# Attention loop of a fused cross-attention and quantised FFN kernel: another order of the steps over four groups in flight

## The chip, the cores and the metric

The kernel runs on one core of a Trainium2 chip. Its time is the device time of one execution, in microseconds (us); a smaller number is better. Five engines take part, each with a queue of its own that it works through: PE (TensorE, matrix products and transposes), DVE (VectorE), ACT (ScalarE), POOL (GpSimd), and SP, which here only issues transfers between HBM and the on-chip memory. Products land in PSUM[...]; everything else on the chip lives in SBUF.

## What is computed

The input `x` has 2 x 2048 tokens of 512 values, the context 2 x 128 tokens. A cross-attention is added to `x`, and then a feed-forward layer whose activations and weights are rounded to integers:

```python
x = x + xattn(layernorm(x), ctx, Wq, Wkv)
x = x + ffn(layernorm(x), w_gate, w_up, w_down)

# xattn: softmax((h @ Wq) @ key.T / sqrt(512)) @ value,  key, value = split(ctx @ Wkv)
# ffn:
x = act_qdq(x)                                  # 16-bit integers, one scale: max |x| over the tensor
up = act_qdq(x @ lpbq_dequant(w_up).T)          # weights: 4 bits in blocks of 32
gate = act_qdq(x @ lpbq_dequant(w_gate).T)
gate = act_qdq(gate * fixed_qdq_u16(sigmoid(gate)))
return act_qdq(gate * up) @ lpbq_dequant(w_down).T
```

The scale of `act_qdq(x)` needs the largest magnitude of the whole normalised tensor, so no product of the FFN can start before the last token has gone through the attention.

## The kernel before

Tokens are worked on in eight groups of 512 (`NG = 8`, `TG = 512`), each held as four tiles of 128 tokens (`NJ = 4`). The program has four stages one after the other: attention (to about 191 us), the gate product (to 469 us), the up product (to 745 us), the down product (from 794 us). This case is about the first.

For one group `g` the attention stage does this. `front` transposes the group's tokens on PE (`xt`, L271) and copies them to SBUF on ACT (`xT`, L272); DVE takes means and variances (L276, L277), and POOL raises them to the power -0.5 (L259). `scores` multiplies with the folded key matrix (`sc`, L288), takes row maxima on DVE (`nmx`, L296, L297), exponentials with row sums on ACT (`e`, L301), and reciprocals of the sums on DVE (`den`, L309). `attend` transposes the exponentials on PE (`pe`, L393), copies them on ACT (`eT`, L395), multiplies with the values (`po`, L399), and adds the result to the tokens on DVE (L400), which also yields row sums (`total`). Then it forms the negative mean on DVE (L411), squares on ACT with row sums (L416), the variance on DVE (L424), its root on POOL (L259) and the shift on DVE (L426). `finish` writes the normalised group `h` on ACT (L433), takes its largest magnitude on DVE (`hmax`, through the helper at L155), transposes it on PE (`ht`, L442) and copies it on ACT (`hT`, L443).

In program order a turn `g` of the loop is: load group `g+2`; scores of `g`; front of `g+1`; three steps of weights; `finish` of `g-1`; `attend` of `g`; three steps of weights. After the loop stands `finish` of group 7.

The "steps of weights" are slices of a generator (`split_weights`, called through `split_rows`) that rounds the gate weights in four blocks of 384 rows. One block is: load (L161), block maxima on DVE (L155), scale and reciprocal (L167, L169), integers (`wi`, L171), back to floats (`w`, L173), three times four transposes on PE and a copy on ACT (`wt`, L179; `wsp`, L180), three splitting operations on DVE (L182, L184, L187) and a store (L189). Six of them take about 1.75 us of DVE each. The same generator works through up and down weights inside the gate stage.

The order of a queue isn't the program's: a scheduler of the language places the instructions of each engine at build time, by priorities and its own estimate of when things are ready. What stands behind what on an engine is therefore read from the built queues. Buffers of the pools are handed out in turn, and a new tile waits until the tile that had its buffer has been read. The PSUM pools of this stage are `ps_t` (two buffers of two banks: `xt`, `ht`), `ps_s` (two of one bank: `sc`, `pe` and `wt`) and `ps_o` (two of one bank: `po`).

After the stage, `over_partitions` reduces `hmax` (L136, POOL L138), `act_scale` makes the scale (L147, L149), group 0 is rounded on DVE (`hi`, L494) and split into the parts of the product (`parts_g`, L221 to L224), while ACT rounds other groups (L500) and makes the first parts (L222). The first matrix product of the gate stage is L479. The last eight of twelve gate weight tiles are loaded at the end of the attention (L471), since their memory is that of the attention's buffers.

Of the kernel before, what the change touches and what calls it, by code (L numbers as in the profile page):

```python
# [62 lines left out]
P = 128  # L63
# [6 lines left out]
EPS = 1e-5  # L70
# [5 lines left out]
def tile_xattn_ffn(  # L76
# [48 lines left out]

    hmax = const.tile([P, NG], F32, name="hmax")
    gmax = const.tile([P, NG * NK], F32, name="gmax")
# [26 lines left out]
    def abs_max(col, src, axis=AX.X):  # L154
        nc.vector.tensor_reduce(col, src, axis, ALU.max, apply_absolute_value=True)  # L155

    def split_weights(pool, psum, src, dst, name):
# [18 lines left out]
        for b in range(3):  # L176
            pt = psum.tile([P, D], F32, tag="tr", name=f"wt_{name}_{b}")
            for c in range(ND):
                nc.tensor.transpose(pt[:, ts(c, P)], w[:, b, ts(c, P)], ident)  # L179
            nc.scalar.copy(ws[:, 2, b, :], pt)  # L180
            yield
# [49 lines left out]
    with ExitStack() as c0:  # L231

        with ExitStack() as c1:
# [20 lines left out]
            nc.gpsimd.memset(mean, 1.0 / D)  # L254
            gate_steps = split_rows(wk1, ps_s, w_gate, wg_d, "g")
            xts = {}
            def inverse_root(ve, name):
                rstd = sm.tile([P, NJ], F32, tag=f"rstd{name[0]}", name=f"rstd_{name}")
                nc.gpsimd.tensor_tensor(rstd, ve, mhalf, ALU.pow)  # L259
                return rstd  # L260

            def front(g):

                xt = xts[g]
                xT = wk2.tile([P, NJ, ND, P], F32, tag="xT", name=f"xT_{g}")
                for j in range(0, NJ, 2):
                    pt = two_banks(f"xt_{g}_{j}")
                    pt4 = pt.rearrange("p (j c k) -> p j c k", j=2, c=ND)
                    for i in range(2):
                        for c in range(ND):  # L270
                            nc.tensor.transpose(pt4[:, i, c, :], xt[:, j + i, ts(c, P)], ident)  # L271
                    nc.scalar.copy(xT[:, j : j + 2], pt4)  # L272
# [7 lines left out]
                return xT, inverse_root(ve, f"x{g}")  # L280

# [104 lines left out]

            def attend(g, e, rden):

                b = g * TG // S
                xt = xts[g]  # L390
                pe = ps_s.tile([P, NJ, P], F32, tag="tr", name=f"pe_{g}")
# [3 lines left out]
                nc.scalar.copy(eT, pe)  # L395
                total = sm.tile([P, NJ], F32, tag="total", name=f"total_{g}")
                for j in range(NJ):
                    po = ps_o.tile([P, D], F32, tag="o", name=f"po_{g}_{j}")
# [9 lines left out]
                    )  # L408
                nc.sync.dma_start(out=x1_d[g], in_=xt)
                nmean = sm.tile([P, NJ], F32, tag="nmean", name=f"nmean_{g}")  # L410
                nc.vector.tensor_scalar(nmean, total, -1.0 / D, None, ALU.mult)  # L411
                h = wk2.tile([P, NJ, D], F32, tag="h", name=f"h_{g}")
                squares = sm.tile([P, NJ], F32, tag="squares", name=f"squares_{g}")
                for j in range(NJ):

# [6 lines left out]
                    )  # L422
                ve = sm.tile([P, NJ], F32, tag="ve2", name=f"ve2_{g}")
                nc.vector.tensor_scalar(ve, squares, 1.0 / D, EPS, ALU.mult, ALU.add)  # L424
                rstd = inverse_root(ve, f"h{g}")
                nc.vector.tensor_tensor(nmean, nmean, rstd, ALU.mult)  # L426
                return h, nmean, rstd

            def finish(g, h, shift, rstd):

                xt = xts.pop(g)
                for j in range(NJ):
                    nc.scalar.activation(  # L433
                        h[:, j, :], xt[:, j, :], AF.Identity, bias=shift[:, j : j + 1], scale=rstd[:, j : j + 1]
                    )
                abs_max(hmax[:, g : g + 1], h, AX.XY)
                for j in range(0, NJ, 2):
# [6 lines left out]

            last = None
            for g in range(NG):
                if g + 2 < NG:
                    xts[g + 2] = load_x(g + 2)
                if g:
                    soft = scores(g, *ahead)  # L450
                if g + 1 < NG:
                    ahead = front(g + 1)
                advance(gate_steps, 3)
                if last is not None:
                    finish(g - 1, *last)
                last = attend(g, *soft)
                advance(gate_steps, 3)
            finish(NG - 1, *last)
            advance(gate_steps, 100)


# [317 lines left out]
```

## Time and profile before

| What | us |
|---|---|
| Median of three runs | 1062.96 (1062.78 to 1064.39) |
| The profiled execution's own time | 1063.58 |
| Its span in the trace | 1061.8 |
| First residual addition of group 0 (L400) | 49.87 |
| End of the last `h` (L433, group 7) | 184.74 |
| First product of the gate stage (L479) | 190.88 |
| First product of the up stage | 470.08 |
| First product of the down stage (L742) | 793.6 |

The squares (L416) of groups 0 to 7 begin at 56.62, 74.34, 93.67, 112.50, 130.59, 149.66, 166.62 and 177.22 us. They serve below as marks of the pace of the loop: each group has exactly one such set, and it stands in the middle of the group's chain.

The profile of one execution is read as follows. A timeline line gives start, duration, engine, line, operation, output and inputs, and in brackets how long the engine stood idle before it and what released it. A windows line gives, for a stretch of time, the busy time of each engine in it with the number of instructions, the clock granted to PE as a share of full speed, and the load of the transfer engines. A waits line adds up how long one kind of instruction let its engine stand idle for another. The three latter stages are bound by PE, which is busy for 271 of the 274 us from 191 to 465 us; the attention stage isn't.

### The profile page before, as it was taken

What the parts mean: (1) busy time and instruction counts of PE and PEld (TensorE: products, weight loads), DVE (VectorE), ACT (ScalarE), POOL (GpSimd) and SP (SyncE); (2) the same over time, 40 slices, a digit from 0 to 9 for tenths busy, and PEclk for the clock granted to TensorE, in tenths of its full rate; (3) what the DMA queues carried; (4) which work ended last, traced back from release to release, by engine and by line L of the source; (5) the groups of instructions that cost most, each with busy time, mean ns of one, the idle gap of its engine ahead of it and who ended that gap; (6) DMA issues with size and microseconds to landing.
All of it is one profiled execution on the core that took longest, in us unless ns stands there. A gap on an engine that the chain in (4) does not pass through costs nothing. (4 is left out here: it accounts for less than half of the span.)

```text
span 1061.8 us, 11414 instructions
## 1 busy us (share of the span) xinstructions
PE 949.2 (89%) x4320; PEld 772.3 (73%) x4320; DVE 793.9 (75%) x897; ACT 542.0 (51%) x582; POOL 72.2 (7%) x63
## 2 busy tenths in 40 slices
PE   6977876899999989999799999999019999999998
PEld 6756663688888878877678888888008888888886
DVE  4577944989998979544777897779458887888782
ACT  2277577532333323225888889888325344443441
POOL 0101010000000000000000000000001112111211
PEclk9988887899999999999899999999559999999999
DMA  8177632977887697887988988889989766766520
GB/s 326 31 291 268 237 135 81 392 304 307 336 351 243 251 328 288 318 323 319 383 286 332 380 319 318 324 323 353 352 269 307 234 196 196 233 190 215 169 76 34
DMA packets 118110, 281.83 MB, mean 265 GB/s; under 512 B 5408, under 2 KB 72992, under 8 KB 105632
## 3 DMA queue, kind: packets, MB, share of 16 engines
q1 hardware_dynamic: 117232, 278.42, 72.0%
q0 software_dynamic: 288, 1.57, 0.4%
q10 hardware_dynamic: 528, 1.05, 0.3%
q8 instruction: 34, 0.56, 0.2%
q14 instruction: 28, 0.23, 0.1%
HBM read 147.85 MB, written 133.17 MB: 265 GB/s over the span
## 5 line engine op out<-in xcount | busy, mean ns | idle before, releaser
L742 PE MATMUL yq<-wd,parts_o 128*128 128x512 f32 x768 | 182.0, 393 | 48.7 <-ACT parts_o L222 48.7
L742 PEld LDWEIGHTS yq<-wd,parts_o 128*128 128x128 f32 x768 | 145.8, 190 | 79.8 <-ACT parts_o L222 49.1
L479 PE MATMUL q_u<-parts_u,wu 128*128 128x512 f32 x768 | 192.4, 393 | 9.8 <-ACT u L595 8.5
L479 PE MATMUL q_g<-parts_g,wg 128*128 128x512 f32 x768 | 195.1, 394 | 4.5 <-ACT parts_g L222 4.5
L479 PEld LDWEIGHTS q_u<-parts_u,wu 128*128 128x128 f32 x768 | 144.7, 189 | 42.8 <-ACT u L595 11.5
L479 PEld LDWEIGHTS q_g<-parts_g,wg 128*128 128x128 f32 x768 | 143.8, 189 | 35.1 <-issue 4.9
L523 ACT ACTIVATE g<-q_g 128x512 f32<-128x512 f32 x96 | 57.5, 601 | 170.6 <-PE q_g L479 165.7
L483 PE MATMUL e_g<-parts_g,wg 128*128 128x512 f32 x384 | 103.6, 391 | 0.0
L483 PE MATMUL e_u<-parts_u,wu 128*128 128x512 f32 x384 | 103.2, 391 | 0.3 <-DVE u L596 0.3
L524 DVE CUSTOM_DVE_ANT_0 g<-g,e_g 128x512 f32<-128x512 f32 x96 | 64.6, 683 | 37.3 <-PE e_g L483 36.9
L746 PE MATMUL ye<-wd,parts_o 128*128 128x512 f32 x384 | 92.2, 389 | 0.0
L588 DVE SCALAR_TENSOR_TENSOR pi<-gi,k_p,sq 128x2048 int16<-128x2048 int16 x24 | 56.3, 2347 | 45.9 <-ACT sq L564 45.9
L483 PEld LDWEIGHTS e_u<-parts_u,wu 128*128 128x128 f32 x384 | 72.5, 189 | 15.9 <-DVE u L596 0.7
L483 PEld LDWEIGHTS e_g<-parts_g,wg 128*128 128x128 f32 x384 | 72.3, 188 | 15.0
L746 PEld LDWEIGHTS ye<-wd,parts_o 128*128 128x128 f32 x384 | 72.1, 188 | 14.9
L750 ACT ACTIVATE yqs<-yq,q_o 128x512 f32<-128x512 f32 x32 | 22.1, 690 | 117.6 <-PE yq L742 117.6
L596 DVE TENSOR_TENSOR u<-u,e_u 128x1024 f32<-128x1024 f32 x48 | 58.5, 1218 | 13.7 <-ACT u L595 13.4
L754 DVE SCALAR_TENSOR_TENSOR y<-ye,e_o,qx 128x512 f32<-128x512 f32 x32 | 24.1, 752 | 57.6 <-PE ye L746 48.3
L752 POOL TENSOR_TENSOR qx<-yqs,x 128x512 f32<-128x512 f32 x32 | 50.0, 1562 | 226.0 <-ACT yqs L750 226.0
L222 ACT CAST parts_o<-sa_o 128x1536 fp32r<-128x1536 int16 x32 | 47.1, 1475 | 34.9 <-PE ye L746 30.8
L595 ACT ACTIVATE u<-q_u 128x1024 f32<-128x1024 f32 x48 | 48.1, 1017 | 31.0 <-PE q_u L479 27.9
L734 DVE SCALAR_TENSOR_TENSOR oi<-p,k_o,ui 128x1536 int16<-128x1536 int16 x32 | 58.0, 1819 | 4.1 <-ACT ui L730 2.2
(165 smaller groups left out, 1293.8 us busy)
## 6 DMA issues: line engine op xcount, KB each, us to landing
parts_d<-parts_g SPq DMA_DIRECT2D x8, 3072.0 KB, 10.9
gate_d<-g SPq DMA_DIRECT2D x24, 1024.0 KB, 5.0
parts_u<-parts_d SPq DMA_DIRECT2D x8, 3072.0 KB, 14.0
gt<-gate_d SPq DMA_DIRECT2D x24, 1024.0 KB, 10.8
up_d<-u SPq DMA_DIRECT2D x24, 1024.0 KB, 6.9
u<-up_d SPq DMA_DIRECT2D x48, 512.0 KB, 6.5
p_d<-pi SPq DMA_DIRECT2D x24, 512.0 KB, 4.6
p<-p_d SPq DMA_DIRECT2D x48, 256.0 KB, 3.9
```

The source lines that it names most:

```text
L222: nc.scalar.copy(parts[:, 0, c], a[:, c])
L479: nc.tensor.matmul(q, lhsT=w[:, s, c, :], rhs=parts[:, s, c, :], start=(c + s == 0), stop=(c + s == ND))
L483: nc.tensor.matmul(e, lhsT=w[:, 2, c, :], rhs=parts[:, 2, c, :], start=(c == 0), stop=(c == ND - 1))
L523: nc.scalar.activation(g4[:, i, :], q, AF.Copy, scale=1.0 + 1.0 / BASE)
L524: nc.vector.tensor_tensor_reduce(g4[:, i, :], g4[:, i, :], e, 1.0, LOWEST, ALU.subtract, ALU.max, gtop[:, m : m + 1])
L588: nc.vector.scalar_tensor_tensor(pi, gi, k_p, sq, ALU.mult, ALU.mult)
L595: nc.scalar.activation(u4[:, i : i + 2, :], q, AF.Copy, scale=1.0 + 1.0 / BASE)
L596: nc.vector.tensor_tensor(u4[:, i : i + 2, :], u4[:, i : i + 2, :], e, ALU.subtract)
L734: nc.vector.scalar_tensor_tensor(oi, pi[:, :, ts(j, P)], k_o, ui[:, :, ts(j, P)], ALU.mult, ALU.mult)
L742: nc.tensor.matmul(q, lhsT=parts[:, s, f, :], rhs=wd[f][:, s, :], start=(f + s == 0), stop=(f + s == NF))
L746: nc.tensor.matmul(e, lhsT=parts[:, 2, f, :], rhs=wd[f][:, 2, :], start=(f == 0), stop=(f == NF - 1))
L752: nc.gpsimd.tensor_tensor(qx, qs, x1[:, j, :], ALU.add)
```

## The change

Only the attention loop and what feeds it are changed; the work on every group is the same. `attend` is taken apart into `turn` (transpose and copy of the exponentials) and a shorter `attend` (products with the values and residual), and the rest of it together with the first half of `finish` becomes `normalise`; the transposes of `h` become `lift`. A turn `i` now works on four groups: `turn` of `i-1` comes first, then scores of `i`, two steps of weights, `attend` of `i-1`, front of `i+1`, two steps of weights, `lift` of `i-2`, `normalise` of `i-1` with its maximum, and two steps of weights. There is one turn more. The last group goes tile by tile of 128 tokens through `attend`, `normalise` and the maximum; `hmax` gets three columns more for it. The PSUM tile of the weight transposes moves from `ps_s` to `ps_o`, where it shares two banks with `po`. The row statistics get tags of their own.

```diff
-    hmax = const.tile([P, NG], F32, name="hmax")
+    hmax = const.tile([P, NG - 1 + NJ], F32, name="hmax")
...
-            pt = psum.tile([P, D], F32, tag="tr", name=f"wt_{name}_{b}")
+            pt = psum.tile([P, D], F32, tag="o", name=f"wt_{name}_{b}")
...
-            gate_steps = split_rows(wk1, ps_s, w_gate, wg_d, "g")
+            gate_steps = split_rows(wk1, ps_o, w_gate, wg_d, "g")
...
-            def inverse_root(ve, name):
-                rstd = sm.tile([P, NJ], F32, tag=f"rstd{name[0]}", name=f"rstd_{name}")
-                nc.gpsimd.tensor_tensor(rstd, ve, mhalf, ALU.pow)
-                return rstd
+            def inverse_root(rstd, ve):
+                nc.gpsimd.tensor_tensor(rstd, ve, mhalf[:, : ve.shape[1]], ALU.pow)
...
-            def attend(g, e, rden):
+            def turn(g, e):
                 pe = ps_s.tile([P, NJ, P], F32, tag="tr", name=f"pe_{g}")
                 for j in range(NJ):
                     nc.tensor.transpose(pe[:, j, :], e[:, j, :], ident)
                 eT = wk2.tile([P, NJ, P], F32, tag="eT", name=f"eT_{g}")
                 nc.scalar.copy(eT, pe)
-                total = sm.tile([P, NJ], F32, tag="total", name=f"total_{g}")
-                for j in range(NJ):
+                return eT
...
+            def attend(g, js, eT, rden, total):
+                b = g * TG // S
+                xt = xts[g]
+                for j in js:
                     po = ps_o.tile([P, D], F32, tag="o", name=f"po_{g}_{j}")
                     nc.tensor.matmul(po, lhsT=eT[:, j, :], rhs=vsb[:, b, :], start=True, stop=True)
                     nc.vector.scalar_tensor_tensor(
...
+            def normalise(g, js, h, total, nmean, squares, ve, rstd):
+                xt = xts[g]
+                w = slice(js[0], js[-1] + 1)
+                nc.vector.tensor_scalar(nmean[:, w], total[:, w], -1.0 / D, None, ALU.mult)
+                for j in js:
                     nc.scalar.activation(
                         h[:, j, :],
...
+                nc.vector.tensor_scalar(ve[:, w], squares[:, w], 1.0 / D, EPS, ALU.mult, ALU.add)
+                inverse_root(rstd[:, w], ve[:, w])
+                nc.vector.tensor_tensor(nmean[:, w], nmean[:, w], rstd[:, w], ALU.mult)
+                for j in js:
                     nc.scalar.activation(
...
+            def lift(g, h):
                 for j in range(0, NJ, 2):
                     pt = two_banks(f"ht_{g}_{j}")
...
-            last = None
-            for g in range(NG):
-                if g + 2 < NG:
-                    xts[g + 2] = load_x(g + 2)
-                if g:
-                    soft = scores(g, *ahead)
-                if g + 1 < NG:
-                    ahead = front(g + 1)
-                advance(gate_steps, 3)
-                if last is not None:
-                    finish(g - 1, *last)
-                last = attend(g, *soft)
-                advance(gate_steps, 3)
-            finish(NG - 1, *last)
+            hs = {}
+            for i in range(NG + 1):
+                if i + 2 < NG:
+                    xts[i + 2] = load_x(i + 2)
+                if i:
+                    eT, rden = turn(i - 1, soft[0]), soft[1]
+                    hs[i - 1] = wk2.tile([P, NJ, D], F32, tag="h", name=f"h_{i - 1}")
+                    rows = row_stats(i - 1)
+                if 0 < i < NG:
+                    soft = scores(i, *ahead)
+                    advance(gate_steps, 2)
+                    attend(i - 1, range(NJ), eT, rden, rows[0])
+                    nc.sync.dma_start(out=x1_d[i - 1], in_=xts[i - 1])
+                if i == NG:
+                    for j in range(NJ):
+                        attend(i - 1, [j], eT, rden, rows[0])
+                    for j in range(NJ):
+                        normalise(i - 1, [j], hs[i - 1], *rows)
+                        abs_max(hmax[:, i - 1 + j : i + j], hs[i - 1][:, j, :])
+                    nc.sync.dma_start(out=x1_d[i - 1], in_=xts[i - 1])
+                if i + 1 < NG:
+                    ahead = front(i + 1)
+                    advance(gate_steps, 2)
+                if i > 1:
+                    lift(i - 2, hs.pop(i - 2))
+                if 0 < i < NG:
+                    normalise(i - 1, range(NJ), hs[i - 1], *rows)
+                    abs_max(hmax[:, i - 1 : i], hs[i - 1], AX.XY)
+                advance(gate_steps, 2)
             advance(gate_steps, 100)
+            lift(NG - 1, hs.pop(NG - 1))
```

More of the change, by code (lines that the diff above doesn't have):

```diff
@@ L279, in front @@
                 nc.vector.tensor_scalar(ve, mv[:, :, 1], EPS, None, ALU.add)
-                return xT, inverse_root(ve, f"x{g}")
+                rstd = sm.tile([P, NJ], F32, tag="rstd", name=f"rstd_{g}")
+                inverse_root(rstd, ve)
+                return xT, rstd
             def scores(g, xT, rstd):
@@ L385, in tile_xattn_ffn @@
             hT = hpool.__enter__().tile([P, ND, NT], F32, name="hT")
-            def attend(g, e, rden):
-                b = g * TG // S
-                xt = xts[g]
+            def turn(g, e):
                 pe = ps_s.tile([P, NJ, P], F32, tag="tr", name=f"pe_{g}")
@@ L395, in attend, with row_stats @@
                 nc.scalar.copy(eT, pe)
-                total = sm.tile([P, NJ], F32, tag="total", name=f"total_{g}")
-                for j in range(NJ):
+                return eT
+            def row_stats(g):
+                return [sm.tile([P, NJ], F32, tag=f"row{i}", name=f"row{i}_{g}") for i in range(5)]
+            def attend(g, js, eT, rden, total):
+                b = g * TG // S
+                xt = xts[g]
+                for j in js:
                     po = ps_o.tile([P, D], F32, tag="o", name=f"po_{g}_{j}")
@@ L408, in attend @@
                     )
[L409 to L414, printed above, removed]
+            def normalise(g, js, h, total, nmean, squares, ve, rstd):
[3 more added lines that the diff above has]
+                for j in js:
                     nc.scalar.activation(
@@ L422, in attend @@
                     )
[L423 to L432, printed above, removed]
+                nc.vector.tensor_scalar(ve[:, w], squares[:, w], 1.0 / D, EPS, ALU.mult, ALU.add)
+                inverse_root(rstd[:, w], ve[:, w])
+                nc.vector.tensor_tensor(nmean[:, w], nmean[:, w], rstd[:, w], ALU.mult)
+                for j in js:
                     nc.scalar.activation(
-                        h[:, j, :], xt[:, j, :], AF.Identity, bias=shift[:, j : j + 1], scale=rstd[:, j : j + 1]
+                        h[:, j, :], xt[:, j, :], AF.Identity, bias=nmean[:, j : j + 1], scale=rstd[:, j : j + 1]
                     )
-                abs_max(hmax[:, g : g + 1], h, AX.XY)
+            def lift(g, h):
                 for j in range(0, NJ, 2):
```

## The prediction

> **What bounds the kernel now.** I read the busy time by stretch first, because the page's average mixes stages with different limits. From 191 us on PE is busy almost throughout, so the change can act only before that. These are four groups of the attention loop, each from the first product of `po` of one group to that of the next, the last row with the tail:
>
> ```profile
> core 0: us, PE busy (x) PEld busy (x) DVE busy (x) ACT busy (x) POOL busy (x), PEclk, DMA share, GB/s
> ...
> 104.92:125.07 20.15, 15.42 (x83) 11.58 (x83) 18.59 (x32) 12.30 (x27) 1.15 (x2) 0.83 0.77 288
> 125.07:143.94 18.87, 16.05 (x104) 13.58 (x103) 13.92 (x27) 13.26 (x28) 2.88 (x3) 0.91 0.20 79
> 143.94:161.62 17.68, 13.71 (x80) 10.68 (x78) 6.79 (x16) 11.85 (x25) 1.01 (x1) 0.90 0.45 175
> 161.62:190.88 29.26, 15.21 (x53) 8.79 (x53) 15.37 (x39) 20.62 (x40) 2.40 (x3) 0.72 0.34 136
> ```
>
> ACT has 12 to 13 us of work in a turn of 18 to 20, DVE 7 to 19. No engine is full over several turns: a chain sets the pace. Next I asked what ACT waits for between 46 and 188 us:
>
> ```profile
> engine line waited for: us in total, times, longest us
> ACT xT L272 <- PE xt L271: 18.2, 4, 6.8
> ACT h L416 <- DVE nmean L411: 10.4, 2, 6.2
> ACT hT L443 <- PE ht L442: 6.3, 9, 1.6
> ```
>
> Then one turn of ACT in order of time (group 4):
>
> ```profile
> 124.42 0.59 ACT L395 COPY eT<-pe 128x512 f32<-128x512 f32 x1
> ...
> 130.59 0.72 ACT L416 ACTIVATE h<-xt,nmean 128x512 f32<-128x512 f32 x1 [4.18 <-DVE nmean L411]
> ...
> 137.03 2.96 ACT L433 ACTIVATE h<-xt,nmean,rstd_h 128x512 f32<-128x512 f32 x4
> 141.04 1.02 ACT L443 COPY hT<-ht 128x1024 f32<-128x1024 f32 x1 [1.05 <-PE ht L442]
> 142.36 1.01 ACT L443 COPY hT<-ht 128x1024 f32<-128x1024 f32 x1 [0.30 <-PE ht L442]
> 143.27 0.59 ACT L395 COPY eT<-pe 128x512 f32<-128x512 f32 x1
> ```
>
> Here the loop closes on itself: 18.85 us from `eT` to the next `eT`. ACT idles 4.18 us while PE multiplies and DVE adds the residual, and 1.35 us for `ht`, because everything from `eT` to `hT` of a group stands in line with nothing of another group to fill the holes. The end of the stage is this:
>
> ```profile
> 184.76 2.29 DVE L155 TENSOR_REDUCE hmax<-h 128x1 f32<-128x2048 f32 x1 [3.06 <-ACT h L433]
> ...
> 186.38 1.01 ACT L443 COPY hT<-ht 128x1024 f32<-128x1024 f32 x1 [0.69 <-PE ht L442]
> ...
> 188.24 2.00 ACT L500 ACTIVATE hi<-hT,r_h 128x2048 int16<-128x2048 f32 x1 [0.85 <-DVE unit L490]
> ```
>
> The last maximum and the last copy of `hT` end within 0.4 us of each other, so shortening one alone gains little.
>
> **What the Trainium skill says.** "Perfetto Trace Analysis", section "Per-engine timelines", has ACT, DVE and POOL as strict FIFOs. The trace agrees: group 0's last residual addition ends at 54.3 us, but its mean (L411) starts at 55.88, after a weight reduction of 1.75 us ahead of it. So it is the order in a queue that counts. "TensorE: Matmul & The Clock Gate", Part 1, says that PE falls to half clock after about 3.4 us of idleness and needs as long to recover. The trace agrees: 16 `ht` transposes take 3.68 us at 182.67, after 6.4 us of idleness, and 16 `xt` transposes 1.91 us at 90.79. "ScalarE: Activation LUTs", section "Table sets", warns of 2.7 us for each change of set; this stage loads one table (1.28 us, at the start) though Exp, Square, Identity and copies alternate, so another mixture of them costs nothing.
>
> **The change, part by part.** Work per group is unchanged. I took the order of each queue from the built program of the changed kernel and laid the durations of before on it by hand: `eT` 0.6, `xT` and `hT` 1.0 a piece, four exponentials 1.75, four squares 2.85, four `h` 2.95, `wsp` 0.6 on ACT; a residual addition 0.72, `hmax` 2.3, `nmx` 0.7, four statistics with aggregates 3.0, a weight operation 1.75 (L182 0.95) on DVE; POOL's root 1.0; `sc` 3.6, eight transposes 0.95, one tile of `po` 1.0 on PE at full clock; about 0.1 for a hand-over.
>
> *The loop.* ACT's queue now reads `eT(g)`, `hT(g-2)`, squares `(g-1)`, `xT`, `h(g-1)`, exponentials `(g+1)`, `eT(g+1)`. The residual chain of a group runs beside the exponentials and copies of another, so the 4.18 us hole closes, and `hT` finds its transposes done. What is late next is DVE, where means stand behind weight operations. An example, between the squares of groups 2 and 3: DVE waits for POOL's root until 97.9 us; then come L182 0.95, residual 0.75, L184 1.75, `hmax` 2.3, two residuals 1.5, L187 1.75, residual 0.75, weight maximum 1.75, mean 0.15, with small ones 11.8 us without a hole, to 109.7. ACT has been out of work since 107.6. The squares begin so (before; worked out for the new order):
>
> group 0: 56.6; 57.9. group 1: 74.3; 76.8. group 2: 93.7; 92.8. group 3: 112.5; 109.8. group 4: 130.6; 126.3. group 5: 149.7; 141.2. group 6: 166.6; 151.4.
>
> The early groups come later, since `eT` of group 1 and 2 run ahead and a weight block stands in front of the means; from group 2 on each turn takes 10 to 17 us instead of 17 to 19. In the turn of group 3 `po` waits for a bank: `wt` now shares `ps_o`, and the second `po` of group 4 can start only after `wsp` at 120.3. That is contained in the 16.5 us of that turn. The weight steps end in the same turn as before, and SP's loads (5.0 us to landing) follow the end of `h` of four groups earlier, more than 5 us ahead of the use but for group 7, which is just in time: 0 to 1 us, taken as 0.
>
> *The tail.* Group 6's squares at 151.4 to 154.25, `eT` of 7 to 154.85, root by 155.7, `h` of 6 to 158.65. On DVE the whole `hmax` of group 6 (158.75 to 161.05) stands before three of group 7's four residuals; these, the fourth product and the means run to 162.7. Then tiles: a square of 0.9, variance, root, shift and `h`. Before, this link took 1.65 us from the last square to `h` once for four tiles (ACT waits so at 181.80); now four times. The root on 128x1 isn't in the trace: between 0.38 (POOL's reduction of 128x1) and 1.01 (128x4); I take 1.01. `h` of the tiles ends at 166.2, 167.5, 170.5 and 171.9, against 184.74: 12.8 us earlier. The last `hmax` is a quarter, about 0.65, which frees DVE 1.65 us sooner; but three copies of `hT` (two of group 7, one left of group 6) now follow `h` on ACT, and the last transposes wait for a PSUM buffer: 1.0 + 1.0 + 2.0 to 175.9, `hi` 2.0, the first parts 0.6, the first product at 178.5 instead of 190.88. Gain 12.4.
>
> *Corrections.* My durations are of a warm PE; before, the granted clock was 0.72 to 1.0 by turn, and cold `sc` costs 3.2 more. I take 2.0 off. The scheduler also placed the weight steps of the gate stage a little differently. There PE has no slack towards weights:
>
> ```profile
> 222.84 1.75 DVE L173 TENSOR_TENSOR w_u<-wi_u,ws_u 128x1536 f32<-128x1536 int16 x1
> ...
> 224.65 1.10 PE L179 MATMUL wt_u<-ident,w_u 128*128 128x128 f32 x8
> ```
>
> PE's transposes follow 0.06 us after L173 ends. In the new order L173 of the first block stands one gate operation (0.61) later; other blocks gain or lose as much. I take 1.0 off, with bounds from a gain of 2.6 (the one stall of this kind before, at 390.75) to a loss of 14 (one operation of 1.75 in each of eight blocks).
>
> Sum against the profiled execution: 1063.58 - 12.4 + 2.0 + 1.0 = 1054.2. The median of the runs lies 0.6 below the profiled one: 1053.6. Up and down stages are the same instructions; their start moves, not their length.
>
> **The rivals.**
> - *A cold PE keeps half of it.* If `sc` leads the path at half clock in three turns, 3 x 3.2 = 9.6 instead of my 2.0: gain 1.8; in two turns 6.4: gain 5.0, 1058. For it: the turn from 48 to 69 us had 0.75. Against: PE works the same 12 us in shorter turns.
> - *The allowances aren't needed*, and the 2.6 us stall of the gate stage goes: 1062.96 - 12.4 - 2.6 = 1048.
> - *The change buys nothing*: DVE has 18.6 us of work in the fullest turn (104.92 to 125.07), so where a weight block falls the chain could still be DVE's, as before: 1063. Against: it is so in three turns only.
> - *Slower: the gate stage stalls on weights.* PE waits in its order for L173 of every block, one DVE operation late each time: 8 x 1.75 = 14.0 against the loop's 10.4, 1066.6. It decides from 1.3 us a block. For it: 0.06 us of slack. Against: the DVE work queued before the first block's L173 is the same in both orders but for 0.61.
>
> **How the numbers follow.** My forecast 1053.6 has 0.58; cold PE 0.20; no allowances 0.07; nothing bought 0.05; slower 0.10. The range must leave out no more than 2 in 10: from 1048.0 to 1060.5. About 2.1 us (0.2%) is what a measurement of this kernel can tell from no change. Faster: 0.58 + 0.20 + 0.07 = 0.85; same: most of "nothing bought", 0.04; slower 0.11.
>
> **What would show it.** Squares of groups 3 and 6 near 110 and 152 us; the idle time of L416 on L411 no longer 4 to 6 us; four roots of 128x1 near 164 to 171; the last `h` near 172 and the first gate product near 178.5; the gate stage again 279 us from there to the first product of the up stage (190.88 to 470.08). Wrong, if the first product comes after 186, or if PE stands in the gate stage for L173.

## The result, and the profile after

The changed kernel takes 1046.68 us (median; 1046.47 to 1047.30), the kernel before on the same chip 1063.68 (1062.78 to 1064.98): a ratio of 0.984 (95% interval 0.9823 to 0.9857). A second measurement on another chip gave 1046.72 and 0.9846 (0.9831 to 0.9861). The forecast was 1053.6, with a range that began at 1048.0: right in direction, too small by 7 us. The span went from 1061.8 to 1045.1 us, that is by 16.7, and so did the profiled execution's own time (1063.58 to 1046.88).

| Mark (us) | Before | Worked out | After |
|---|---|---|---|
| Squares of group 0 begin | 56.62 | 57.9 | 57.12 |
| of group 1 | 74.34 | 76.8 | 75.27 |
| of group 2 | 93.67 | 92.8 | 90.18 |
| of group 3 | 112.50 | 109.8 | 107.64 |
| of group 4 | 130.59 | 126.3 | 123.82 |
| of group 5 | 149.66 | 141.2 | 138.58 |
| of group 6 | 166.62 | 151.4 | 148.87 |
| End of the last `h` | 184.74 | 171.9 | 167.57 |
| First product of the gate stage | 190.88 | 178.5 | 175.71 |
| First product of the up stage | 470.08 | 458.7 | 453.68 |

The column "worked out" is the replay alone, without the 2.0 us for a cold PE; its last entry is 178.5 plus the old length of the gate stage, 279.2, plus the 1.0 that the prediction allowed for that stage. Of the 16.7 us the attention stage gave 15.2, the gate stage 1.2 (279.20 to 277.97), the up stage 0.3; the down stage starts at 776.92 instead of 793.61 and is no shorter.

First the busy time by stretch of the kernel after; each stretch goes from the squares of one group to those of the next (groups 2 to 6).

```profile
core 0: us, PE busy (x) PEld busy (x) DVE busy (x) ACT busy (x) POOL busy (x), PEclk, DMA share, GB/s
...
90.18:107.64 17.46, 14.35 (x67) 9.67 (x68) 14.92 (x30) 13.32 (x29) 3.13 (x3) 0.80 0.57 200
107.64:123.82 16.18, 13.82 (x91) 10.24 (x91) 12.85 (x29) 12.89 (x29) 3.46 (x2) 1.00 0.60 224
123.82:138.58 14.76, 12.07 (x77) 8.92 (x77) 13.34 (x27) 12.20 (x28) 2.50 (x2) 1.00 0.65 250
138.58:148.87 10.29, 8.97 (x51) 5.76 (x50) 6.53 (x15) 9.44 (x23) 1.97 (x2) 1.00 0.40 165
```

A turn takes 10 to 17 us, and ACT still has 9 to 13 us of work in it. The same view over the whole loop, squares of group 0 to squares of group 6, before and then after:

```profile
56.62:166.62 110.00, 85.95 (x481) 66.23 (x481) 77.79 (x152) 76.15 (x167) 11.42 (x10) 0.86 0.58 217
```
```profile
57.12:148.87 91.75, 77.99 (x468) 56.36 (x466) 76.04 (x148) 73.06 (x157) 13.06 (x10) 0.96 0.70 263
```

DVE and ACT do nearly the same work (77.8 and 76.0; 76.2 and 73.1 us) in 18.25 us less. PE is busy 8 us less, at a granted clock of 0.96 instead of 0.86. So no work went away: holes did. ACT's waits between 46 and 180 us show which:

```profile
engine line waited for: us in total, times, longest us
ACT hT L447 <- PE ht L446: 8.3, 5, 2.3
ACT xT L271 <- PE xt L270: 6.5, 4, 5.1
ACT h L424 <- DVE row L421: 4.9, 3, 2.5
ACT h L435 <- DVE row L433: 4.1, 5, 1.2
```

The wait for `xt` fell from 18.2 to 6.5, that for the mean (L416 before, now L424) from 10.4 to 4.9, with 2.5 as its longest instead of 6.2. The wait for `ht` did not fall (6.3 before, 8.3 now); part of it now stands in the tail. One turn of ACT from `eT` to `eT`, group 4 again:

```profile
121.11 0.59 ACT L394 COPY eT<-pe 128x512 f32<-128x512 f32 x1
123.25 0.59 ACT L180 COPY wsp_g<-wt_g 128x512 f32<-128x512 f32 x1 [1.55 <-PE wt_g L179]
123.82 0.72 ACT L424 ACTIVATE h<-xt,row 128x512 f32<-128x512 f32 x1
...
128.93 0.46 ACT L302 ACTIVATE e<-sc,nmx,rstd 128x128 f32<-128x128 f32 x1 [1.70 <-PE xt L270]
...
131.66 2.93 ACT L435 ACTIVATE h<-xt,row,row 128x512 f32<-128x512 f32 x4 [0.86 <-DVE row L433]
134.50 1.90 ACT L271 COPY xT<-xt 128x1024 f32<-128x1024 f32 x2
136.29 0.58 ACT L394 COPY eT<-pe 128x512 f32<-128x512 f32 x1
```

15.2 us instead of 18.85. Ahead of the squares stand 1.55 us of waiting for a weight's transposes instead of 4.18 for the mean, and the copies of `hT`, which stood between `h` and the next `eT`, have left this chain: those of an earlier group follow at 136.77, without a wait. At the end of the stage:

```profile
156.41 2.29 DVE L155 TENSOR_REDUCE hmax<-h 128x1 f32<-128x2048 f32 x1 [1.21 <-ACT h L435]
...
160.14 0.72 ACT L424 ACTIVATE h<-xt,row 128x512 f32<-128x512 f32 x1 [0.47 <-DVE row L421]
...
165.93 0.54 POOL L259 TENSOR_TENSOR row<-row,mhalf 128x1 f32<-128x1 f32 x1 [0.34 <-DVE row L431]
...
168.33 0.17 DVE L136 TENSOR_REDUCE m_h<-hmax 128x1 f32<-128x11 f32 x1
...
170.53 1.01 ACT L447 COPY hT<-ht 128x1024 f32<-128x1024 f32 x1 [1.15 <-PE ht L446]
172.22 0.38 POOL L138 PARTITION_ALL_REDUCE a_h<-m_h  x1 [5.74 <-issue]
172.63 0.15 DVE L147 TENSOR_SCALAR s_h<-a_h 128x1 f32<-128x1 f32 x1 [4.13 <-POOL a_h L138]
...
173.07 2.00 ACT L522 ACTIVATE hi<-hT,r_h 128x2048 int16<-128x2048 f32 x1 [1.52 <-DMA wg<-wg_d]
```

The maximum of group 6 stands on DVE ahead of group 7's residuals, as expected. New is the last wait. `m_h` is ready at 168.50, yet POOL's reduction of it starts at 172.22, and nothing in the trace releases it. ACT's `hi` waits 1.5 us after the last `hT`. The record names a weight load, but what `hi` needs and lacks is the scale: it starts when `unit`, three small operations after `a_h`, is done. Before, the same gap was there (a root at 180.50, the reduction at 187.38) and hid behind the last maximum, which ended `m_h` at 187.25.

### The profile page after: what moved, and what is told of

Same layout as the page of the kernel before. It is cut to its first block, busy times and chain, and to the rows that moved or that the text cites. A ratio compares the mean times of both kernels' runs of the same rounds, so it can differ in the third digit from the quotient of the medians.

```text
span 1045.1 us, 11428 instructions
## 1 busy us (share of the span) xinstructions
PE 944.2 (90%) x4320; PEld 764.4 (73%) x4320; DVE 796.2 (76%) x909; ACT 541.9 (52%) x582; POOL 75.2 (7%) x66
## 3 DMA queue, kind: packets, MB, share of 16 engines
q10 hardware_dynamic: 528, 1.05, 0.3%
## 5 line engine op out<-in xcount | busy, mean ns | idle before, releaser
L764 PE MATMUL yq<-wd,parts_o 128*128 128x512 f32 x768 | 182.0, 393 | 48.6 <-DMA u<-up_d 48.6
L222 ACT CAST parts_o<-sa_o 128x1536 fp32r<-128x1536 int16 x32 | 47.1, 1474 | 35.8 <-PE ye L768 31.6
```

The costliest lines, as they stand in the source:

```text
L222: nc.scalar.copy(parts[:, 0, c], a[:, c])
L764: nc.tensor.matmul(q, lhsT=parts[:, s, f, :], rhs=wd[f][:, s, :], start=(f + s == 0), stop=(f + s == NF))
```

## The experiments

Ratios are to the kernel before on the same chip (its medians there: 1063.68 to 1064.52). The loop (group 0's squares) began at 57 to 61 us in these kernels, so the table gives the first gate product and also its distance from group 0's first square. "Gate" is the length of the gate stage.

In five kernels (e1, e2, e10, e11, e14) 1.7 us of a late beginning are the clock's. Between 24 and 32 us PE was granted 0.79 of full speed in them and 1.00 in the eleven others, and the same 30 products took longer. The first of them in the kernel after (21 in 4.80 us) and in e1 (13 in 4.70):

```profile
25.48 4.80 PE L361 MATMUL pg<-kT,wqT 128*128 128x256 f32 x21 [1.34 <-DVE kT L355]
```
```profile
25.60 4.70 PE L361 MATMUL pg<-kT,wqT 128*128 128x256 f32 x13 [2.19 <-DVE kT L355]
```

PE begins the products after these (`pm`) at 31.6 to 31.9 us in the eleven and at 33.3 to 33.5 in the five. For these 1.7 us the distance from the mark is the fairer measure. Any other lateness may belong to the edit, and then the distance hides it.

| Kernel | Time, us | Ratio (95%) | First product | From group 0's squares | Gate |
|---|---|---|---|---|---|
| before | 1063.68 | 1 | 190.88 | 134.26 | 279.2 |
| after | 1046.68 | 0.9840 (0.9823–0.9857) | 175.71 | 118.59 | 278.0 |
| e1_whole_last | 1050.66 | 0.9874 (0.9857–0.9890) | 176.76 | 117.89 | 281.2 |
| e2_tiles_only | 1061.54 | 0.9973 (0.9963–0.9983) | 192.02 | 133.56 | 277.8 |
| e3_wt_bank | 1050.27 | 0.9873 (0.9857–0.9889) | 178.57 | 120.90 | 277.5 |
| e4_lift_soon | 1050.42 | 0.9875 (0.9859–0.9892) | 178.32 | 120.96 | 277.5 |
| e5_turn_late | 1048.97 | 0.9859 (0.9844–0.9874) | 177.55 | 120.58 | 276.9 |
| e6_max_on_pe | 1051.23 | 0.9883 (0.9867–0.9899) | 176.74 | 119.51 | 278.8 |
| e7_hmax6_late | 1044.26 | 0.9819 (0.9806–0.9832) | 173.54 | 116.34 | 277.5 |
| e8_both | 1044.70 | 0.9822 (0.9809–0.9836) | 172.00 | 114.88 | 278.1 |
| e9_reduce_early | 1048.42 | 0.9855 (0.9840–0.9870) | 176.00 | 118.79 | 278.3 |
| e10_both_early | 1045.00 | 0.9820 (0.9807–0.9834) | 175.43 | 116.53 | 277.6 |
| e11_no_third | 1043.03 | 0.9805 (0.9787–0.9822) | 174.23 | 114.78 | 276.8 |
| e12_after_again | 1046.72 | 0.9846 (0.9831–0.9861) | 175.24 | 118.15 | 277.9 |
| e13_three_undone | 1057.48 | 0.9939 (0.9922–0.9955) | 186.41 | 126.76 | 278.2 |
| e14_four_undone | 1059.96 | 0.9962 (0.9949–0.9976) | 187.60 | 126.32 | 281.1 |

**Which part carries the gain?** Four kernels, each with one part undone or alone.

The last group whole again (e1):

```diff
-                    for j in range(NJ):
-                        attend(i - 1, [j], eT, rden, rows[0])
-                    for j in range(NJ):
-                        normalise(i - 1, [j], hs[i - 1], *rows)
-                        abs_max(hmax[:, i - 1 + j : i + j], hs[i - 1][:, j, :])
+                    attend(i - 1, range(NJ), eT, rden, rows[0])
+                    normalise(i - 1, range(NJ), hs[i - 1], *rows)
+                    abs_max(hmax[:, i - 1 : i], hs[i - 1], AX.XY)
```

> The changed kernel, but the last group goes through attend, normalise and the maximum as a whole. Theory 'loop' (the gain is the loop's: squares of group 6 at 148.9 instead of 166.6, and the tail gives some back): the last h ends at about the same time (squares 160.1, four of them 2.85, link 1.65, four h 2.95: 167.6), the maximum takes 1.6 more, so 1045 to 1049 us. Rival 'tiles' (the last group in tiles brings a third or more of the 17 us): 1052 us or more.

The time, 1050.66, lies between the two bands. The first product came 1.05 us later, with a loop that began 1.75 later, by the clock. From group 6's squares to the first product it took 26.86 us (26.84 with the tiles). So the tiles did not shorten the attention measurably. The other 3.2 us of this kernel's loss lie in the gate stage, where nothing was edited (below).

The kernel before with the last group in tiles (e2):

```diff
+                if g == NG - 1:
...
+                    for j in range(NJ):
+                        normalise_tile(g, j, h, total, nmean, squares, ve, rstd)
+                    return h, nmean, rstd
```

> The kernel before with one part of the change alone: its last group is squared, normalised and reduced tile by tile. Theory 'loop': 1062 to 1066 us, no gain. Rival 'tiles': 1058 us or less.

The time, 1061.54, is just below the first band. 0.7 us came in the attention from group 0 on, behind a loop that began 1.8 later, and 1.4 in the gate stage: alone, the tiles are worth almost nothing to the attention.

The transposes of the weights back in the banks of the scores (e3):

```diff
-            pt = psum.tile([P, D], F32, tag="o", name=f"wt_{name}_{b}")
+            pt = psum.tile([P, D], F32, tag="tr", name=f"wt_{name}_{b}")
...
-            gate_steps = split_rows(wk1, ps_o, w_gate, wg_d, "g")
+            gate_steps = split_rows(wk1, ps_s, w_gate, wg_d, "g")
```

> The changed kernel with the weight transposes' PSUM tile back in the pool of sc and pe. Theory 'loop': the order does the work, the bank little, 1045 to 1051 us, a little slower because pe and sc wait for wsp. Rival 'bank' (pe and sc no longer waiting for wsp copies is what lets eT run ahead): 1055 us or more.

2.9 us lost at the first product, 2.3 from group 0 on: the bank is no main part. That the loss is the bank's at all isn't shown. All of it stands in the turn from group 0's squares to group 1's (21.0 us instead of 18.2), and there the granted clock was 0.84 instead of 1.00.

`h` transposed in the turn of its normalisation (e4):

```diff
-                if i > 1:
-                    lift(i - 2, hs.pop(i - 2))
                 if 0 < i < NG:
                     normalise(i - 1, range(NJ), hs[i - 1], *rows)
                     abs_max(hmax[:, i - 1 : i], hs[i - 1], AX.XY)
+                    lift(i - 1, hs.pop(i - 1))
```

> The changed kernel with h transposed right after its normalisation in the same turn, not two turns after its exponentials. If the late lift is a main part of the gain (ACT no longer waits for ht after h, 1.35 us a turn before, and eT is no longer behind it): 1052 to 1058 us. If turning the exponentials first is enough: 1046 to 1050 us.

2.6 and 2.4 us, with a time just above the band of the second theory. Later, the exponentials transposed at the head of their residual chain (e5):

```diff
-                    eT, rden = turn(i - 1, soft[0]), soft[1]
+                    now = soft
...
                     advance(gate_steps, 2)
+                    eT, rden = turn(i - 1, now[0]), now[1]
                     attend(i - 1, range(NJ), eT, rden, rows[0])
```

> After, but the exponentials are transposed where the residual chain begins (after the scores of the next group and two steps of weights), not first in the turn. Theory 'loop' (having several groups in flight carries the gain, no single place of a step): the first gate product at 176 to 180, i.e. at most 4 us of the 15.2 us of the attention stage are lost. Rival 'transposed first' (eT early on ACT's queue is what closes the hole of 4.18 us per turn): the squares of the middle groups fall back by 2 to 4 us a turn, first product near 186 to 191.

1.8 and 2.0 us. The squares of group 4 fell back by 4.2 us (127.99), but not by 2 to 4 in every turn. No single part is "the" change. The three named parts sum to 6.7 us from group 0 on, of 15.7 gained, so all three were undone together (the three diffs above, e13), then the tiles too (e14):

> After, with three parts undone at once: wt back in the banks of the scores, h transposed directly after its normalisation, exponentials transposed at the head of their residual chain; tiles for the last group stay, and so does the place of the residual chain, one turn after the scores. Alone they cost 2.9, 2.6 and 1.8 us at the first gate product. Theory 'the residual chain one turn later carries the rest': about their sum, 182 to 184. Theory 'the parts cover for each other': 187 to 191, the time of the kernel before.

> As the run before it, and the last group as a whole too. What is left of the change is the residual chain of a group one turn later, after the scores of the next, the weight steps in pairs, and the separate tags. Theory 'residual chain one turn later': first gate product at 183 to 186, squares of group 6 near 158 to 160. Theory 'the parts cover for each other': squares of group 6 at 163 to 167 and the first product at 188 to 192.

The first products, 186.41 and 187.60, fell between the two bands and just outside the second theory's; the squares of group 6, at 163.75 in the second, are in its band. The loss is 10.7 us, and 11.9 or, without the 1.7 us of the clock, 10.2: more than the 7.3 that the three edits cost singly. So the parts cover for each other in part. Some 4.5 to 5 of the 15.2 us remain at the first product. From group 0's squares on it is more, 7.5 and 7.9 of 15.7, but that leaves out 2.5 us by which both loops begin late without the clock being slower there. What remains lies in what none of these edits touched: the residual chain behind the next group's scores, the pairing of weight steps, the separate tags. Which of them was not tried alone. Most of the loss stands early. From group 0's squares to group 2's the two take 38.2 and 38.9 us (33.1 in the kernel after), at a clock of 0.80 and 0.86 in the turn of group 1 (1.00); from there to the first product 88.6 and 87.4 (85.5; before, 97.2). How much of the early loss is the slower clock's stays open. ACT's waits of the first of the two kernels between 46 and 180 us:

```profile
engine line waited for: us in total, times, longest us
ACT eT L394 <- PE pe L392: 12.1, 5, 6.4
ACT h L424 <- DVE row L421: 9.7, 4, 4.1
```

The hole ahead of the squares is back at its old size (9.7 us; 10.4 before), and `eT` now waits 12.1 us for its transposes (1.9 before).

**Does DVE's order set the pace now?** The last splitting operation is left out for the gate weights, so this kernel (e11) does not compute the right products:

```diff
-        nc.vector.scalar_tensor_tensor(ws[:, 2], ws[:, 0], 1.0 + 1.0 / BASE, ws[:, 2], ALU.mult, ALU.subtract)
+        if name[0] != "g":
+            nc.vector.scalar_tensor_tensor(ws[:, 2], ws[:, 0], 1.0 + 1.0 / BASE, ws[:, 2], ALU.mult, ALU.subtract)
```

> After, without the last of the three splitting operations (L187, 1.75 us on DVE) in the four blocks of gate weights, so that the gate product is made with one wrong part of the weights; nothing else is left out, and the other steps keep their turns. It takes four times 1.75 = 7.0 us of work from DVE. Theory 'DVE's order sets the pace' (the means of a group stand behind weight operations): where such an operation stands ahead of a mean, as between the squares of groups 2 and 3, the turn shortens by about 1.7 us; first gate product 4 to 7 us sooner than the changed kernel's 175.7. Rival 'ACT or PE sets it now' (ACT is busy for 12 to 13 us of a turn of 15 to 17 and only one chain passes through DVE): less than 1.5 us in all.

The first product came only 1.5 us sooner, at the rival's edge. But this loop began at 59.45 (57.12), 1.7 us of it by the clock; without these it would be some 3 us, between the two bands. The scheduler also placed things differently: one weight operation (L171, 1.75 us at 57.59) now stands ahead of group 0's mean, where in the kernel after it follows it. One of the four left-out operations stood ahead of the loop (49.98 us). The loop from group 0's squares to group 6's:

```profile
59.45:146.95 87.50, 75.50 (x459) 55.57 (x458) 68.53 (x143) 72.55 (x156) 11.51 (x10) 0.96 0.72 254
```

DVE has 7.5 us less work between the marks (68.53, not 76.04), most of it three left-out operations and the one that moved. The loop is 4.25 us shorter (87.50, not 91.75). So a little over half of what is taken from DVE comes off the path. Its queue is part of what sets the pace; that it alone does is not shown.

**What ends the attention stage?** Two POOL records of the kernel after, by line, stand right behind the last root, which ends at 166.47, and ahead of the late reduction:

```profile
L138 POOLq MODIFY_POOL_CONFIG  x2: 11/11/11, 166.4 to 166.5; - x2
```

The Trainium skill ("GPSIMD Engine Reference", section "Instruction dispatch") says that the first call to a freshly loaded kernel of POOL pays about 6 us (5.95 measured there) that no instruction shows. The gap here is 5.74. If it is paid once, an early call hides it (e9):

```diff
+    first = const.tile([P, NJ], F32, name="first")
+    nc.gpsimd.partition_all_reduce(first, mhalf, P, bass_isa.ReduceOp.max)
```

> After, plus one reduction over the partitions of a constant at the very start of POOL's queue (its result is not used). In the changed kernel POOL's reduction a_h starts 5.74 us after POOL's last root, although the maximum m_h that it reads was ready 3.7 us earlier; the trace shows two MODIFY_POOL_CONFIG of 11 ns just ahead of it, and none ahead of the two later reductions of the same line. Theory A (one load of code, paid by whichever reduction comes first): the gap moves to the start, where POOL is idle to 16.3 us; a_h follows m_h within 0.2 us, near 168.6; then ACT's hi starts when hT is there, 171.5 to 171.7 instead of 173.1; first gate product near 174.2, 1.5 us sooner; time about 1.5 us below the changed kernel's. Theory B (a switch from the root to the reduction, paid each time the kind of work changes): a_h still starts 5.4 to 5.9 us after the last root and the first product stays at 175.7.

POOL's timeline of this kernel:

```profile
11.07 0.39 POOL L116 PARTITION_ALL_REDUCE first<-mhalf  x1 [9.41 <-issue]
...
22.44 1.14 POOL L261 TENSOR_TENSOR rstd<-ve,mhalf 128x4 f32<-128x4 f32 x1 [10.84 <-issue]
...
166.16 0.54 POOL L261 TENSOR_TENSOR row<-row,mhalf 128x1 f32<-128x1 f32 x1 [0.34 <-DVE row L433]
172.51 0.38 POOL L140 PARTITION_ALL_REDUCE a_h<-m_h  x1 [5.81 <-issue]
```

Theory B holds. POOL idles 9.41 us ahead of the early reduction (more than ahead of the late ones; why is not shown), a MEMSET after it (11.33) doesn't wait, the first root after it comes 6.1 us later than in the kernel after (16.32), and the last reduction waits again, 5.81. The price comes back with the change from root to reduction; it isn't that of a first call in the program. For the way back there is this one clean case.

The reduction was then made without POOL, by PE and DVE (e6):

```diff
-            s_h, r_h = act_scale(*over_partitions(hmax, name="h"), "h")
+            m_h = const.tile([P, 1], F32, name="m_h")
+            nc.vector.tensor_reduce(m_h, hmax, AX.X, ALU.max)
+            a_h = const.tile([P, 1], F32, name="a_h")
+            with tc.tile_pool(name="ps_h", bufs=1, space=PSUM) as ps_h:
+                all_h = ps_h.tile([P, P], F32, name="all_h")
+                nc.tensor.transpose(all_h, m_h.to_broadcast([P, P]), ident)
+                nc.vector.tensor_reduce(a_h, all_h, AX.X, ALU.max)
+            s_h, r_h = act_scale(a_h, "h")
```

> After, but the largest magnitude over the partitions is made by one transpose on PE and one maximum on DVE from PSUM in place of POOL's reduction. Theory 'POOL's change from root to reduction (5.7 us) ends last': hi of ACT starts when hT is there, 171.5 to 171.8 instead of 173.1; first gate product near 174.2, 1.5 us sooner. Rival 'hT and the weight load end together with it': no more than 0.5 us.

From group 7's squares to the first product it took 15.34 us; the kernel after took 15.57, and 15.33 in its second profile. The number is the rival's, but the run doesn't decide, because the scale came no sooner:

```profile
169.59 0.16 DVE L510 TENSOR_REDUCE m_h<-hmax 128x1 f32<-128x11 f32 x1
...
171.79 1.01 ACT L447 COPY hT<-ht 128x1024 f32<-128x1024 f32 x1 [1.14 <-PE ht L446]
172.85 0.48 PE L514 MATMUL all_h<-ident,m_h 128*128 128x128 f32 x1 [1.10 <-ACT hT L447]
...
174.13 2.00 ACT L529 ACTIVATE hi<-hT,r_h 128x2048 int16<-128x2048 f32 x1 [1.33 <-DVE unit L519]
```

`m_h` is ready at 169.75, but the transpose that spreads it stands on PE behind the last transposes of `h` and then waits for the last copy of `hT`. It starts 3.1 us later, and ACT's `hi` waits 1.33 us for the scale (1.52 in the kernel after). (The median is 4.5 us above the changed kernel's on the same chip, 1051.23 and 1046.72. Between the two profiled executions it is 2.7: 1.4 from group 0's squares to the first product, where the turn of group 1 met the slower products of the last section, and 0.9 in the gate stage, with a stall of 2.3 instead of 0.7.)

The maximum of group 6 behind the roots of group 7, held there by a one-column copy that reads the last root's row (e7):

```diff
+                    nc.vector.tensor_copy(hmax[:, i - 2 : i - 1], rows[4][:, NJ - 1 :])
+                    abs_max(hmax[:, i - 2 : i - 1], h6, AX.XY)
...
+                if 0 < i < NG - 1:
                     abs_max(hmax[:, i - 1 : i], hs[i - 1], AX.XY)
+                if i == NG - 1:
+                    h6 = hs[i - 1]
```

> After, but DVE's maximum of group 6 is ordered behind the roots of group 7, so that it no longer stands between the residuals of group 7. Same sum of work plus one copy of 128x1. Theory 'order on DVE sets the tail': squares of group 7 begin near 157.5 instead of 160.1, the last h ends near 164 instead of 167.6, and the first gate product comes at 171.5 to 172.5 instead of 175.7, 3 to 4 us sooner; what is late next is POOL's reduction (last root plus 5.7 us) and hT together. Rival 'ACT and PE set the tail' (products of group 7 and squares queue behind ACT's h of group 6): last h moves by less than 1 us and the first product by less than 1 us.

The squares of group 7 began at 156.42 (160.14), the last `h` ended at 165.32 (167.57), and the first product came at 173.54: 2.2 us, not 3 to 4. POOL and ACT in this kernel:

```profile
163.68 0.54 POOL L259 TENSOR_TENSOR row<-row,mhalf 128x1 f32<-128x1 f32 x1 [2.46 <-DVE row L431]
170.06 0.38 POOL L138 PARTITION_ALL_REDUCE a_h<-m_h  x1 [5.84 <-issue]
```
```profile
166.53 1.01 ACT L447 COPY hT<-ht 128x1024 f32<-128x1024 f32 x1 [0.30 <-PE ht L446]
170.91 2.00 ACT L527 ACTIVATE hi<-hT,r_h 128x2048 int16<-128x2048 f32 x1 [3.37 <-DMA wg<-wg_d]
```

ACT now waits 3.37 us for the scale, although the last `hT` is there at 167.54 and `m_h` at 167.59: POOL's change of work ends the stage. Adding the early reduction to it (e10)

> The two edits together: an early reduction at the start of POOL's queue, and the maximum of group 6 behind the roots of group 7. If both reasons hold, the last h ends near 164, m_h near 166.5, a_h directly after it, and hi waits for hT alone (168.0): first gate product 170.3 to 171.5, about 4.5 to 5 us sooner than in the changed kernel; time near 1042 against 1046.7 of the changed kernel, if the gate stage keeps its 278 us (it varied from 277.5 to 281.2 with the order of the weight steps). If only one reason holds, it equals the better of the two single edits within 0.3 us.

brought nothing (116.53 us from group 0 on, against 116.34; its loop began 1.7 later, by the clock), as follows from theory B. Adding the maximum on PE (e8) did, at the first product:

> After, with the maximum over the partitions on PE and DVE, and the maximum of group 6 behind the roots of group 7. With the latter alone the last h ended at 165.3 and the first product came at 173.5, ACT's hi waiting 3.4 us for the scale. If POOL's change of work is all that holds hi there, the first product comes at 170.2 to 171.0, 4.7 to 5.5 us sooner than in the changed kernel, and the time is near 1041.5 (both kernels beaten) with a gate stage of 277.5 to 278. If transposes of h hold it too, 172 to 173.

`a_h` is there at 168.9 instead of 170.4, `hi` starts at 169.39, and the first product comes at 172.00. That is 1.5 us on top, though short of 170.2 to 171.0: in the turn of group 1 this loop lost 1.3 us (76.52, not 75.27) to slower products on PE (last section). It is not `hT` that holds `hi` now, as the last band would have it: the last copy ends at 167.95, and ACT waits 1.44 us for the scale. Here the transpose of `m_h` follows it at once, since the copies are done. The total shows none of the 1.5 us: in the profiled executions the gate stage is 0.6 and the down stage 1.2 us longer than with the late maximum alone. Its time, 1044.70 (1044.32 to 1045.95), and that of the late maximum alone, 1044.26 (1043.95 to 1045.83), can be set against the changed kernel run once more, on the same chip as the first of the two:

> The changed kernel as it is, on the same chip as the three others, so that they can be compared with it directly. All theories: 1046 to 1048.5, first gate product 175.5 to 176.2.

It took 1046.72 (1046.27 to 1048.83), with its first product at 175.24. Every run of the two lies below every run of it, and their medians are 2.0 and 2.5 us lower: both beat both kernels, the late maximum alone by a comparison across two chips, though the intervals of the ratios still touch.

## Why the prediction fell short

The sum missed 7.3 us against the profiled execution (1054.2 and 1046.88): 2.8 at the first product, 2.0 and 1.0 for the two corrections, 1.2 that the gate stage gained instead, 0.3 of the up stage. So the mechanism was right, and two steps failed: the corrections took 3.0 off where nothing was lost, and the replay of the first three groups was 2.6 too long.

**Right: the cause and the chain.** The hole of 4.18 us closed, and DVE is late next, though it sets the pace only in part (e11). The stretch worked out as 11.8 us of DVE without a hole, from the root of group 2 to the mean of group 3, is in the trace from 95.57 to 107.60, 12.0 us, in the order told, with one hole of 0.96. It began 2.3 us earlier than worked out.

**Slightly off: the early groups.** All 2.5 us of the loop's miss are there by group 2 (92.8 and 90.18); from there to group 6 the replay is within 0.5. Of it, 0.8 was at group 0 and another 0.75 at group 1. Which durations were too long there isn't shown.

**Not needed, and for the gate stage wrong in sign: "Corrections".** *Cold PE, 2.0 taken off.* The replay had used durations of a warm PE, and the loop got one: clock 0.96, 1.00 in three of the four turns shown. The allowance carried over the clock of before (0.72 to 1.0), which went with the idle time that the change removes. That the shorter idle time keeps the clock up was not tested alone. *Gate stage, 1.0 taken off.* The stage gained 1.2. PE's stall, in the kernel after and in the one with the last group whole:

```profile
375.20 1.07 PE L179 MATMUL wt_d<-ident,w_d 128*128 128x128 f32 x8 [0.74 <-issue]
```
```profile
377.40 1.94 PE L179 MATMUL wt_d<-ident,w_d 128*128 128x128 f32 x8 [2.59 <-issue]
```

It was 2.62 before. The stalls explain 1.9 of the 3.2 us between these two; PE was also busy 1.4 us longer. In the kernels of the table the stage takes 276.8 to 281.2 us with the same number of matrix products. That it is the scheduler's placing of the weight steps is likely, not shown: the record names no releaser for the stall. The bounds (gain 2.6, loss 14) were far too wide on one side. The rival "The allowances aren't needed" (0.07, 1048) came nearest, and it should have been the forecast.

**Right in sum by luck, two errors against each other: "The tail".** From group 6's squares to the first product 27.1 us were worked out and 26.84 came. The root on 128x1 takes 0.54 to 0.55, not the 1.01 taken (bounds 0.38 and 1.01); with four of them, the stretch from group 7's squares to the last `h` took 7.43 instead of 9.2. POOL's 5.74 us then gave most of that back: 8.14 instead of 6.6 from the last `h` to the first product. The trace of before shows the gap, put down to `m_h`, which ended 0.1 us ahead of the reduction; the prediction had no term for it.

**The rivals that fell.** Cold PE (1058), nothing bought (1063), slower by stalls of the gate stage (1066.6): `w_u` and `w_d` cost no more than before. One reading was too broad without harm: PE is not busy throughout from 191 us on. Between the up and the down product it stands idle for 48.6 us, in both kernels.

## What to carry to other kernels

When the order of a loop changes, replay the built queues by hand with measured durations; an allowance for a slow clock that had been measured amid the idle time about to vanish was not needed here. Undo parts singly and together, measure at the end of the stage and from a mark inside it, and compare the granted clock by stretch before an edit is given a loss of 2 us. When a step is moved to another engine to test whether it ends last, look whether it really came sooner. Ahead of the last reduction of a stage, look for an idle gap that ends only just after its input: what hides there becomes the bound when the input comes earlier.

## What was not expected of the hardware

POOL's change from a root (`pow`) to a reduction over the partitions took 5.4 to 6.2 us in each of the kernels that make it, with no busy instruction in the trace; the way back took about 6.1 in the one case that shows it. Later reductions with no root between show no such gap: they start when their input is there. And the clock can change a turn without any change in its queue. These are the same four products of group 0, after the same 1.19 us of idleness, in the kernel after and in the one with the maximum on PE:

```profile
67.79 1.88 PE L406 MATMUL po<-vsb,eT 128*128 128x512 f32 x4
```
```profile
67.90 3.24 PE L406 MATMUL po<-vsb,eT 128*128 128x512 f32 x4
```

The granted clock between 64 and 70 us was 1.00 in the first and 0.86 in the second, and the squares of group 1 came at 75.27 and 76.74. PE had not idled longer than 1.19 us at a stretch since 28 us in either, so the 3.4 us of idleness that the prediction quotes are not needed for a slower clock. What tips it, with PE's queue the same to 0.1 us up to there, stays open.
